# A fused attention and transformer kernel: where the softmax maximum is injected, how probabilities are stored, and leaner first-stage copies

## The chip, the cores and the metric

The kernel runs on one core of one Trainium2 chip. The metric is the time of one execution on the device in microseconds (us), the median of three runs. A profile is one further execution, recorded by the hardware profiler; its span runs from the first to the last instruction of the program.

The engines' names are as in the profile: PE is the matrix engine's matmuls and PEld its weight loads, DVE the vector engine, ACT the scalar engine (activations), POOL the GpSimd engine, SP the engine that issues the DMAs.

## The reference

The input x is 16 sequences of 256 tokens with 128 features. Two residual blocks follow each other. The first is one windowed attention (windows of 64 tokens, 16 heads of 8 features). The second is six layers, each of an attention (16 heads of 64 features, windows of 32 that look back at one window) and a feed-forward part with a gated gelu. Cut to what matters here:

```
x = x + first_attention(layernorm(x))          # _L0_attn_ref
    q, k = layernorm over the 8 features of a head;  softmax(q k^T) v;  W_proj, b_proj
x = x + six_layers(layernorm(x))               # _L0_ffn_ref
    for i in range(6):
        s = shift_tokens(x)                    # half of the features from the token before
        q, k, v = s @ Wqkv[i];  q, k = l2norm, scaled;  rotary tables
        p = softmax(8 * q k^T, masked to the window and the one before)
        x = (p v) @ Wo[i] + x
        s = layernorm(shift_tokens(x))
        x = (a * gelu(gate)) @ W2[i] + b2[i] + x      # a, gate = split(s @ W1[i] + b1[i])
```

## The kernel before

**Two stages.** `first_attention` computes the first block for all sequences and leaves the result, normalised and transposed, in `xg` in SBUF. Then the layers run, 6 x 32 tiles of 128 tokens, in one software pipeline.

**The pipeline of the layers.** Each tile passes through stages, and in turn t the kernel works on several tiles at once: `stage_p` (projections) on tile t, `stage_s` (scores) on t-1, `stage_e` (exponentials) on t-2, `stage_v` (probabilities times values) on t-3, `stage_w` (output projection) on t-5, and pieces of `stage_f` (feed-forward, one unit of two sequences in four turns) behind. Every stage is a generator that is cut into steps, and each step has a place in the turn between 0 and 1 (`AT_P`, `AT_E`, `AT_V`, `AT_W`, `AT_S`, `AT_F`, `AT_L`, lines 27 to 30). `merge_at` runs the steps sorted by place; equal places go in the order of the list of stages. `mul` (line 291) and `flip` (line 294) issue every matmul and transpose of the layers and pin each behind the one before, so that the order of the matrix engine is exactly this order. The other engines' orders are chosen when the program is built, by the priority of the program's order and by a model of when inputs are ready; they are in-order queues on the chip.

**The steps of a turn**, with the names used here:
- P0 to P5: the six projections (q, k in P0 to P3, k first; v in P4 and P5), each three matmuls, with four transposes among them that `turned` has queued: k and q of tile t-1 in P0 to P3, the probabilities p of tile t-2 in P4 and P5. Each projection takes a PSUM bank of the pool `p`, which has two; in P0 to P3 DVE multiplies it with the rotary tables (line 643), ACT squares it (line 652), then DVE reduces (653), and POOL adds and scales (654, 660, 664).
- S at .72: a mask matmul and 128 score matmuls into two banks of the pool `s` (two banks), then on DVE the negated row maxima `nm` (line 738).
- E at .2 and .21 of the next turn: a matmul per bank adds the maxima to the scores, and ACT writes the exponentials to `p` (one buffer, line 275 through `tab`).
- P4, P5 then transpose `p`, and ACT copies it to `pt` (line 621), one buffer of 8 x 128 columns, the half `mb` at a time.
- V1 at .1 and V2 at .45 of the turn after: 64 small matmuls each. V1 takes its two banks from the pool of four (`t`, `w`, `f`), V2 from the pool of the scores (`USE_V`). DVE takes reciprocals and multiplies (790, 791), ACT casts (795), POOL subtracts (796), and a DMA transposes the result.
- W at .47: 24 matmuls, added to `xg` by DVE (817).
- Feed-forward steps: Fc and Fo (centring and variance), six Fp (three gelus, three products), F2 (second matrix, added to `xg` by DVE, 895), and in the last layer `emit_out`: eight transposes of `xg` per unit into two banks of the pool `p`, each half added on DVE (834) to the residual. Before the gelus and after them ACT loads another table.

The order on the matrix engine around the change, in a turn without feed-forward steps, is S, P5, then P0, V1, P1, E, P2, V2, W, P3, P4.

**The first attention.** Eight units of 512 tokens pass `stage_load`, `stage_qkv`, `stage_heads`, `stage_soft`, `stage_out`, `stage_norm`, merged in a similar manner, but without pins. The lines that the change touches: `row_stats` sums rows by ACT (line 320, each with a read of the accumulator) for the units' first statistics (`a`) and the last ones (`b`); `rv` (370) is on DVE; `stage_heads` splits q and k into a high and a low half-precision part by ACT (414) and POOL (415) and doubles both by a DVE copy (417, 419) before a DMA transpose; `stage_out` fills one bank per half c of the rows (480), with a reciprocal (482) and two multiplications (485) each. Its five PSUM pools have 2, 2, 2, 1, 1 banks.

Of the kernel before, what the change touches and what calls it, by code (L numbers as in the profile page):

```python
# [10 lines left out]
F32 = mybir.dt.float32  # L11
# [3 lines left out]
AF = mybir.ActivationFunctionType  # L15
ALU = mybir.AluOpType
AX = mybir.AxisListType
# [7 lines left out]
KT = 2  # L25
LAG_S, LAG_P, LAG_V, LAG_W = 1, 2, 3, 5
AT_P = tuple(c / 6 for c in range(6))
AT_E, AT_V, AT_W, AT_S = (0.2, 0.21), (0.1, 0.45), (0.47,), (0.72,)
AT_F = ((0.86,), (0.06, 0.74, 0.88), (0.03, 0.27, 0.8), (0.1, 0.35, 0.6))
AT_L = 0.71  # L30
LOAD_AT = 6
LOAD_T = 10
SPLIT = (2, 4, 2)
SPLIT0 = (2, 2, 2, 1, 1)
USE = dict(p=0, t=1, w=1, f=1, s=2)
USE_V = (1, 2)
LQ0, LH0, LS0, LO0, LN0 = 2, 4, 6, 7, 9
# [11 lines left out]
VPRE = 16.0  # L49
# [6 lines left out]
def kernel(  # L56
# [233 lines left out]
    def mul(*args, **how):  # L290
        pin(T.matmul(*args, **how))  # L291
# [5 lines left out]
    def first_attention(p1, p2, p3, pqp, psp0, pop, pyp, ptp=None):  # L297
# [17 lines left out]
        def row_stats(xt, pre):  # L315
            mu = p3.tile([128, 4], F32, name=f"{pre}mu")
            rs = p3.tile([128, 4], F32, name=f"{pre}rs")
            sq = p3.tile([128, 128], F32, name="sq0")
            for t in range(4):
                S.activation(sq, xt[:, t], AF.Copy, scale=-1.0 / 128.0, accum_out=mu[:, t : t + 1])  # L320
            for t in range(4):
                S.activation(sq, xt[:, t], AF.Square, bias=mu[:, t : t + 1], accum_out=rs[:, t : t + 1])
            rsqrt(rs, rs, 1.0 / 128.0)
            return mu, rs
# [39 lines left out]
        def stage_load(u):  # L364
            if u:
                load_x(u)
            e = U[u]
            _, e.rs = row_stats(e.xt, "a")
            e.rv = p1.tile([128, 4], F32, name="rv")
            V.tensor_scalar(e.rv, e.rs, VPRE, None, ALU.mult)  # L370
            yield
            e.xnt = p1.tile([128, 2, 4, 128], FR, name="xnt")
            pt = ptp.tile([128, 4, 128], F32, name="pt" if ptp is not pyp else "py")
            for t in range(4):
                T.transpose(pt[:, t], e.xt[:, t], ident)
            S.copy(e.xnt[:, 0], pt)
            V.tensor_tensor(e.xnt[:, 1], pt, e.xnt[:, 0].bitcast(F32), ALU.subtract)
            G.tensor_tensor(e.xt, e.xt, bpt.unsqueeze(1).to_broadcast([128, 4, 128]), ALU.add)
            yield
# [26 lines left out]
        def stage_heads(u):  # L406
            e = U[u]
            e.hl = []
            for s in range(2):
                src = e.qk[:, :, s * 128 : s * 128 + 128].rearrange("p t (h d) -> p t h d", d=8)  # L410
                hl = p1.tile([128, 4, 16, 4, 8], HP, name=f"hl{s}")
                for t in range(4):
                    hi, lo = hl[:, t, :, 0], hl[:, t, :, 2 if s else 1]
                    S.copy(hi, src[:, t])
                    G.tensor_tensor(lo, src[:, t], hi, ALU.subtract)
                    if s:
                        V.tensor_copy(hl[:, t, :, 1:4:2], hl[:, t, :, 0:3:2])
                    else:
                        V.tensor_copy(hl[:, t, :, 2:4], hl[:, t, :, 0:2])
                tr = p2.tile([128, 4, 4, 128], HP, name=f"tr{s}")  # L420
                nc.sync.dma_start_transpose(
                    tr.rearrange("p t i q -> p (t i) q"), hl.rearrange("p t h a d -> p (t h a d)")
                )
                e.hl.append(tr)
                yield
# [41 lines left out]
        def stage_out(u, n2):  # L467
            e = U[u]
            for n in range(2):
                t = 2 * n2 + n  # L470
                pt0 = e.pt[n]
                v = v0[(4 * u + t) % NV0]
                o0 = p3.tile([128, 2, 8, 8], F32, name="o0")
                for c in range(2):
                    r = slice(64 * c, 64 * c + 64)
                    po = pop.tile([128, 8, 18], F32, name="po")
                    for gm in range(8):
                        p = gm % 4 * 2 + gm // 4
                        for q, (a, b) in enumerate(((0, 0), (0, 1), (1, 0))):
                            T.matmul(po[:, p], pt0[r, a * 8 + gm], v[r, b, p], start=(q == 0), stop=(q == 2))  # L480
                    rc = p3.tile([128, 8], F32, name="rc0")
                    V.reciprocal(rc, po[:, :, 16])
                    for hp in range(2):
                        h = slice(64 * hp, 64 * hp + 64)
                        V.tensor_tensor(
                            o0[h, c],
                            po[h, :, hp * 8 : hp * 8 + 8],
                            rc[h].unsqueeze(2).to_broadcast([64, 8, 8]),
                            ALU.mult,
                        )  # L490
                yield
                py = pyp.tile([128, 512], F32, name="py")
                T.transpose(py[:, 0:128], o0.rearrange("p c a b -> p (c a b)"), ident)
                ot0 = p3.tile([128, 128], F32, name="ot0")
                S.copy(ot0, py[:, 0:128])
                py = pyp.tile([128, 512], F32, name="py")
                for c in range(2):
                    r = slice(64 * c, 64 * c + 64)
                    for hp in range(2):
                        T.matmul(  # L500
                            py[r, 0:128],
                            ot0[r, hp * 64 : hp * 64 + 64],
                            wp[r, hp],
                            start=(hp == 0),
                            stop=(hp == 1),
                        )
                V.scalar_tensor_tensor(e.xt[:, t], py[:, 0:128], 1.0 / VPRE, e.xt[:, t], ALU.mult, ALU.add)
                yield
# [49 lines left out]
    def bank(kind):  # L558
        n = USE.get(kind, kind)
        return banks[n].tile([128, 512], F32, name=f"bank{n}")  # L560
# [47 lines left out]
    def turned(src, dst, mb):  # L608
        hold = []

        def one(m):
            if m == 0:
                hold.append(bank("t").rearrange("p (m q) -> p m q", q=128))
            flip(hold[0][:, m], src(m), ident)
            if m == 3:
                to = dst
                if isinstance(dst, Tl):
                    if mb == 0:
                        dst.pt = work.tile([128, 8, 128], F32, name="pt", bufs=1)
                    to = dst.pt  # L620
                S.copy(to[:, mb * 4 : mb * 4 + 4], hold[0])  # L621

        turns.extend((lambda m=m: one(m)) for m in range(4))

# [63 lines left out]
    def line_up(t):  # L688
        if 0 <= t - LAG_S < total:
            d = tiles[t - LAG_S]  # L690
            if d.j == 0:
                kts[0] = front.tile([128, 8, 256], F32, name="kt", bufs=KT)
            d.ktp = kts[0]
            d.kt = d.ktp[:, :, 128 - 128 * d.j : 256 - 128 * d.j]
            d.qt = front.tile([128, 8, 128], F32, name="qt", bufs=2)
            for s, dst in ((1, d.kt), (0, d.qt)):
                for hb in range(2):
                    nat = d.nat[s][hb].rearrange("p (m a) d -> p m (a d)", a=2)
                    turned(lambda m, nat=nat: nat[:, m], dst, hb)
        if 0 <= t - LAG_P < total:  # L700
            d = tiles[t - LAG_P]
            for mb in range(2):
                turned(lambda m, mb=mb: d.p[:, mb * 4 + m].rearrange("p a k -> p (a k)"), d, mb)

# [60 lines left out]
    def stage_v(t):  # L765
        d = tiles[t]
# [11 lines left out]
        for mb in range(2):  # L778
            po = [bank(USE_V[mb])[:, 0:260].rearrange("p (m d) -> p m d", d=65) for a in range(2)]
            for m in range(4):  # L780
                for s in range(4):
                    for a in range(2):
                        r = slice(64 * a, 64 * a + 64)
                        q = slice(32 * s, 32 * s + 32)
                        mm = mb * 4 + m
                        mul(po[a][q, m], d.pt[r, mm, q], vv[s, a][r, mm], start=True, stop=True)
            of = work.tile([128, 4, 2, 64], F32, name="of", bufs=2)
            for a in range(2):
                rc = work.tile([128, 4], F32, name="rc", bufs=4)
# [30 lines left out]
    def emit_out(b, nb):  # L820
        g, k = divmod(b, GB)
        n = 2 * nb
# [4 lines left out]
        yt = pool.tile([128, 12 if name == "gt" else 4, 128], F32, name=name, bufs=bufs)[:, 0:n]  # L827
        for a in range(2):
            r = slice(64 * a, 64 * a + 64)
            pm = bank("p")[:, 0:256].rearrange("p (t c) -> p t c", c=64)[:, 0:n]  # L830
            for t in range(n):
                c0 = t % 2 * 128 + a
                flip(pm[:, t], xg[g][r, k + t // 2, c0 : c0 + 128], ident[r, r])
            V.tensor_tensor(yt[:, :, r], pm, r1[:, :, r], ALU.add)  # L834
# [187 lines left out]
```

## Time and profile before

| What | us |
|---|---|
| median of three runs (3214.35 to 3215.15) | 3214.44 |
| the profiled execution, its own time | 3213.12 |
| its span, first to last instruction | 3211.3 |
| first attention: start to the first scores of the layers | about 287 |
| first to last exponential of the layers | 293.3 to 3168.7 |
| TensorE clock granted, mean over the span | 0.957 |

The page has a line for each engine (busy time, share of the span, instructions) and rows of digits in which the span is cut into 40 slices: a digit is the busy share in tenths, and in the row PEclk the share of the clock that was granted. A busy time of the matrix engine is modelled at its ends and can hide short waits; therefore starts are compared in what follows. In a list of instructions the last bracket gives the idle time of the engine before it and who ended it.

### The profile page before, as it was taken

To read this page: it belongs to the slowest core of one execution; us is meant where nothing else is said; L and a number is where in the kernel's file an instruction comes from. 1 tells how busy PE (TensorE), PEld (TensorE's weight loads), DVE (VectorE), ACT (ScalarE), POOL (GpSimd) and SP (SyncE) were. 2 spreads that over 40 slices of the span, in tenths; PEclk is the share of its full clock that TensorE was granted. 3 is DMA by queue.
4 is the path that set the end of the run, shared out by engine and by line. 5 is a ranking of instruction groups with operands and counts; after the bars stand their busy time and mean duration, and the time that the engine had idled before them with its cause. 6 is when DMAs were issued, how large, how long until landed. Compare 5 with 4: busy or idle time off the path is not lost. (4 is left out here: it accounts for less than half of the span.)

```text
span 3211.3 us, 153330 instructions
## 1 busy us (share of the span) xinstructions
PE 2994.2 (93%) x67106; PEld 2099.0 (65%) x67106; DVE 2583.3 (80%) x4850; ACT 2384.4 (74%) x5034; POOL 2510.2 (78%) x2578
## 2 busy tenths in 40 slices
PE   4887999999999999999999999999999999999997
PEld 3655766666666666666666666666666666666664
DVE  7987888887788887788887788887788887787774
ACT  6877777777777777777777777777777777776774
POOL 5656988888888788888788888788888788887772
PEclk6558999999999999999999999999999999999998
DMA  4763545444444434444444444444444444443433
GB/s 109 134 130 86 101 96 106 89 85 88 93 95 107 87 87 88 93 95 105 89 87 86 94 96 104 89 88 84 95 98 103 89 89 81 95 93 91 89 89 71
DMA packets 622945, 302.98 MB, mean 94 GB/s; under 512 B 533446, under 2 KB 545732, under 8 KB 622276
## 3 DMA queue, kind: packets, MB, share of 16 engines
q1 hardware_dynamic: 622276, 293.18, 43.5%
q8 instruction: 528, 8.65, 1.1%
q14 instruction: 141, 1.16, 0.1%
HBM read 22.45 MB, written 4.19 MB: 8 GB/s over the span
## 5 line engine op out<-in xcount | busy, mean ns | idle before, releaser
L291 PE MATMUL bank<-wqkv,xhl 128*128 128x512 f16 x3456 | 1234.4, 380 | 10.0 <-ACT sq L652 9.3
L654 POOL TENSOR_TENSOR sum<-mc 128x512 f32<-128x512 f32 x768 | 995.8, 1300 | 230.4 <-DVE mc L643 211.3
L643 DVE TENSOR_TENSOR mc<-bank,tq 128x1024 f32<-128x1024 f32 x768 | 928.2, 1218 | 148.3 <-PE bank L294 135.4
L664 POOL TENSOR_TENSOR sum<-sum,r 128x512 f32<-128x512 f32 x768 | 796.2, 1058 | 31.9
L653 DVE TENSOR_REDUCE r<-sq 128x8 f32<-128x512 f32 x768 | 520.4, 683 | 277.4 <-ACT sq L652 267.4
L294 PE MATMUL bank<-ident,sum 128*128 128x128 f32 x3072 | 710.5, 273 | 0.0
L796 POOL TENSOR_TENSOR ohl<-of,ohl 128x512 f16<-128x512 f32 x384 | 451.7, 1176 | 211.5 <-ACT ohl L795 210.8
L652 ACT ACTIVATE sq<-bank 128x512 f32<-128x512 f32 x768 | 459.6, 608 | 160.4 <-DVE mc L643 158.7
L294 PEld LDWEIGHTS bank<-ident,sum 128*128 128x128 f32 x3072 | 432.4, 141 | 131.8 <-issue 13.9
L291 PEld LDWEIGHTS <-xhl 128*128 128x128 f16 x3456 | 337.6, 98 | 191.0 <-issue 18.5
L795 ACT CAST ohl<-of 128x512 f16<-128x512 f32 x384 | 237.8, 619 | 269.5 <-DVE of L791 266.8
L291 PE MATMUL bank<-vb,pt 64*32 64x65 f32 x6144 | 376.0, 225 | 50.9 <-ACT p L275 26.4
L291 PEld LDWEIGHTS bank<-vb,pt 64*32 64x32 f32 x6144 | 257.0, 105 | 218.6 <-ACT p L275 75.1
L294 PE MATMUL bank<-ident,p 128*128 128x128 f32 x1536 | 355.0, 273 | 0.1
L291 PE MATMUL bank<-v,pt 64*32 64x65 f32 x6144 | 312.6, 224 | 39.4 <-ACT p L275 17.8
L291 PE MATMUL bank<-vw,pt 64*32 64x65 f32 x12288 | 331.8, 225 | 1.2 <-issue 1.0
L791 DVE TENSOR_TENSOR of<-bank,rc 128x256 f32<-128x256 f32 x768 | 295.4, 416 | 1.7
L291 PE MATMUL bank<-ot,wohl 128*128 128x128 f16 x4608 | 292.0, 220 | 2.0 <-issue 1.1
L291 PEld LDWEIGHTS bank<-kt,qt 64*32 64x32 f32 x24576 | 255.4, 105 | 44.4 <-issue 44.1
L291 PE MATMUL bank<-kt,qt 64*32 64x64 f32 (+1 forms) x24576 | 283.7, 223 | 0.3 <-issue 0.2
L291 PEld LDWEIGHTS bank<-v,pt 64*32 64x32 f32 x6144 | 235.2, 105 | 70.5 <-ACT p L275 33.2
L291 PEld LDWEIGHTS <-wohl 128*128 128x128 f16 x4608 | 259.1, 98 | 21.0 <-issue 3.1
(155 smaller groups left out, 5033.9 us busy)
## 6 DMA issues: line engine op xcount, KB each, us to landing
v<-vb SPq DMA_DIRECT2D x384, 130.0 KB
vw<-vb SPq DMA_DIRECT2D x384, 130.0 KB
vw<-vb SPq DMA_DIRECT2D x576, 65.0 KB
wraw<-in_L_ffn_Wqkv_dram SPq DMA_DIRECT2D x36, 256.0 KB
wraw<-in_L_ffn_Wo_dram SPq DMA_DIRECT2D x12, 256.0 KB
ot<-ohl SPq DMA_TRANSPOSE x192
xt<-in_L_attn_x_dram SPq DMA_DIRECT2D x8, 256.0 KB
r1d<-xt SPq DMA_DIRECT2D x8, 256.0 KB
```

The source lines that it names most:

```text
L291: pin(T.matmul(*args, **how))
L294: pin(T.transpose(*args))
L643: V.tensor_tensor(prod, p4.unsqueeze(3).to_broadcast([128, 8, 2, 2, 32]), tq[:, s, d.j].unsqueeze(1).to_broadcast([128, 8, 2, 2, 32]), ALU ...
L652: S.activation(sq, pp.rearrange("p (h d) -> p h d", d=64), AF.Square)
L653: V.tensor_reduce(r[:, hb * 8 : hb * 8 + 8], sq, AX.X, ALU.add)
L654: G.tensor_tensor(mc, m2[:, :, 0], m2[:, :, 1], ALU.add)
L664: G.tensor_tensor(mc, mc, rb.unsqueeze(2).to_broadcast([128, 8, 64]), ALU.mult)
L791: V.tensor_tensor(of[:, :, a], po[a][:, :, 0:64], rc.unsqueeze(2).to_broadcast([128, 4, 64]), ALU.mult)
L795: S.copy(ohl[:, 0, h], of)
L796: G.tensor_tensor(ohl[:, 1, h], of, ohl[:, 0, h], ALU.subtract)
```

## The change

Six edits:
- the places of `stage_e` go from .2 and .21 to .09 and .095, which is before V1 (.1) and behind the feed-forward steps at .03 and .06;
- `pt` becomes two tiles of four times 128 columns, `pt0` and `pt1`, one buffer each;
- `emit_out` takes its banks from the pool of four;
- `stage_heads` writes high and low parts at double width by ACT and POOL, and the DVE copies are gone;
- `stage_out` uses one tile of two banks for both halves c, with the matmuls of the two halves alternating, one reciprocal and two multiplications over both; the pool has one such tile, and the pools' counts are 2, 2, 1, 1, 1;
- the last statistics (`b`) take their sums by one DVE reduction and a small POOL multiplication, and `rv` moves from DVE to POOL.

```diff
-AT_E, AT_V, AT_W, AT_S = (0.2, 0.21), (0.1, 0.45), (0.47,), (0.72,)
+AT_E, AT_V, AT_W, AT_S = (0.09, 0.095), (0.1, 0.45), (0.47,), (0.72,)
...
-SPLIT0 = (2, 2, 2, 1, 1)
+SPLIT0 = (2, 2, 1, 1, 1)
...
-            for t in range(4):
-                S.activation(sq, xt[:, t], AF.Copy, scale=-1.0 / 128.0, accum_out=mu[:, t : t + 1])
+            if pre == "a":
+                for t in range(4):
+                    S.activation(sq, xt[:, t], AF.Copy, scale=-1.0 / 128.0, accum_out=mu[:, t : t + 1])
+            else:
+                V.tensor_reduce(mu, xt, AX.X, ALU.add)
+                G.tensor_scalar(mu, mu, -1.0 / 128.0, None, ALU.mult)
...
-            V.tensor_scalar(e.rv, e.rs, VPRE, None, ALU.mult)
+            G.tensor_scalar(e.rv, e.rs, VPRE, None, ALU.mult)
...
+                hi, lo = (slice(0, 2), slice(2, 4)) if s else (slice(0, 3, 2), slice(1, 4, 2))
                 for t in range(4):
-                    hi, lo = hl[:, t, :, 0], hl[:, t, :, 2 if s else 1]
-                    S.copy(hi, src[:, t])
-                    G.tensor_tensor(lo, src[:, t], hi, ALU.subtract)
-                    if s:
-                        V.tensor_copy(hl[:, t, :, 1:4:2], hl[:, t, :, 0:3:2])
-                    else:
-                        V.tensor_copy(hl[:, t, :, 2:4], hl[:, t, :, 0:2])
+                    two = src[:, t].unsqueeze(2).to_broadcast([128, 16, 2, 8])
+                    S.copy(hl[:, t, :, hi], two)
+                    G.tensor_tensor(hl[:, t, :, lo], two, hl[:, t, :, hi], ALU.subtract)
...
-                for c in range(2):
-                    r = slice(64 * c, 64 * c + 64)
-                    po = pop.tile([128, 8, 18], F32, name="po")
...
+                both = pop.tile([128, 2, 512], F32, name="po")
+                po = both[:, :, 0:144].rearrange("p c (m e) -> p c m e", e=18)
+                for gm in range(8):
+                    p = gm % 4 * 2 + gm // 4
+                    for q, (a, b) in enumerate(((0, 0), (0, 1), (1, 0))):
+                        for c in range(2):
+                            r = slice(64 * c, 64 * c + 64)
+                            T.matmul(po[:, c, p], pt0[r, a * 8 + gm], v[r, b, p], start=(q == 0), stop=(q == 2))
+                rc = p3.tile([128, 2, 8], F32, name="rc0")
+                V.reciprocal(rc, po[:, :, :, 16])
+                for hp in range(2):
+                    h = slice(64 * hp, 64 * hp + 64)
+                    V.tensor_tensor(
+                        o0[h],
+                        po[h, :, :, hp * 8 : hp * 8 + 8],
+                        rc[h].unsqueeze(3).to_broadcast([64, 2, 8, 8]),
+                        ALU.mult,
+                    )
...
-                    if mb == 0:
-                        dst.pt = work.tile([128, 8, 128], F32, name="pt", bufs=1)
-                    to = dst.pt
-                S.copy(to[:, mb * 4 : mb * 4 + 4], hold[0])
+                    dst.pt[mb] = work.tile([128, 4, 128], F32, name=f"pt{mb}", bufs=1)
+                    S.copy(dst.pt[mb], hold[0])
+                else:
+                    S.copy(dst[:, mb * 4 : mb * 4 + 4], hold[0])
...
-                        mul(po[a][q, m], d.pt[r, mm, q], vv[s, a][r, mm], start=True, stop=True)
+                        mul(po[a][q, m], d.pt[mb][r, m, q], vv[s, a][r, mm], start=True, stop=True)
...
-            pm = bank("p")[:, 0:256].rearrange("p (t c) -> p t c", c=64)[:, 0:n]
+            pm = bank("t")[:, 0:256].rearrange("p (t c) -> p t c", c=64)[:, 0:n]
```

More of the change, by code (lines that the diff above doesn't have):

```diff
@@ L473, in stage_out @@
                 o0 = p3.tile([128, 2, 8, 8], F32, name="o0")
-                for c in range(2):
-                    r = slice(64 * c, 64 * c + 64)
-                    po = pop.tile([128, 8, 18], F32, name="po")
[L477 to L490, printed above, removed]
+                both = pop.tile([128, 2, 512], F32, name="po")
[16 more added lines that the diff above has]
+                    )
                 yield
@@ L615, in one @@
             if m == 3:
-                to = dst
                 if isinstance(dst, Tl):
-                    if mb == 0:
-                        dst.pt = work.tile([128, 8, 128], F32, name="pt", bufs=1)
-                    to = dst.pt
-                S.copy(to[:, mb * 4 : mb * 4 + 4], hold[0])
+                    dst.pt[mb] = work.tile([128, 4, 128], F32, name=f"pt{mb}", bufs=1)
+                    S.copy(dst.pt[mb], hold[0])
+                else:
+                    S.copy(dst[:, mb * 4 : mb * 4 + 4], hold[0])
         turns.extend((lambda m=m: one(m)) for m in range(4))
@@ L701, in line_up @@
             d = tiles[t - LAG_P]
+            d.pt = [None, None]
             for mb in range(2):
```

## The prediction

> **What bounds the kernel now.** I read the page first, then stretches cut at turns, then the waits, then the engines' instructions in order of time.
>
> ```profile
> PE 2994.2 (93%) x67106; PEld 2099.0 (65%) x67106; DVE 2583.3 (80%) x4850; ACT 2384.4 (74%) x5034; POOL 2510.2 (78%) x2578
> PEclk6558999999999999999999999999999999999998
> ```
>
> TensorE is near full from slice 5 on, at the full granted clock; in the first three and a half slices (the first attention) it has about half the clock and is not full. So there are two stages with two limits. Here are four successive turns of the layers, cut where S (the scores) ends: a plain one, one with Fc/Fo, one with gelus, one with F2 (columns: stretch, length, busy us and count of PE, PEld, DVE, ACT, POOL, clock, DMA share, GB/s).
>
> ```profile
> 1567.57:1580.69 13.12, 12.96 (x342) 10.03 (x333) 12.01 (x23) 9.65 (x21) 11.07 (x13) 1.00 0.55 94
> 1580.69:1595.57 14.88, 14.21 (x336) 9.77 (x331) 12.30 (x23) 11.20 (x24) 11.15 (x12) 1.00 0.46 92
> 1595.57:1613.02 17.45, 16.08 (x351) 10.83 (x341) 11.92 (x22) 14.85 (x29) 14.33 (x16) 1.00 0.38 81
> 1613.02:1629.62 16.60, 16.60 (x350) 11.56 (x345) 15.55 (x28) 9.88 (x21) 12.97 (x13) 1.00 0.47 90
> ```
>
> DVE leaves 1.1 us free in the plain turn and in the F2 turn, 2.6 and 5.5 in the others. TensorE's order is written out, so a stall of it lengthens the turn at once. The waits between 300 and 3165 us say what it stalls on (in all, times, longest):
>
> ```profile
> PEld bank L291 <- ACT p L275: 104.5, 237, 0.7
> PEld bank L291 <- ACT pt L621: 45.4, 52, 1.0
> PE bank L294 <- DVE gt L834: 9.4, 6, 1.6
> ```
>
> The first is V2: its two banks come from the pool of the scores and are free only when both exponentials (p, L275) have read them. One such case, in the Fc turn, ScalarE then TensorE:
>
> ```profile
> 1587.14 0.59 ACT L621 COPY kt<-bank 128x512 f32<-128x512 f32 x1 [0.29 <-PE bank L294]
> 1587.83 0.62 ACT L865 CAST xnhl<-gt 128x512 f16<-128x512 f32 x1
> 1588.35 1.08 ACT L275 ACTIVATE p<-bank 128x512 f32<-128x512 f32 x2
> ```
> ```profile
> 1586.94 0.59 PE L291 MATMUL bank<-nm,identh 128*128 128x512 f16 x2
> 1587.37 0.38 PE L291 MATMUL bank<-wqkv,xhl 128*128 128x512 f16 x1
> ...
> 1588.99 0.30 PE L291 MATMUL bank<-vb,pt 64*32 64x65 f32 x2 [0.37 <-ACT p L275]
> ...
> 1590.26 1.51 PE L291 MATMUL bank<-ot,wohl 128*128 128x128 f16 x24
> ```
>
> E is issued at 1586.94, its exponentials end at 1589.43, and V2 starts only with the first (1588.99) and takes 1.27 us.
>
> To count the stalls I took, for each block of TensorE, the distance from its start to the next block's start, less the short distance that recurs for it: P 1.09, V 0.79, E 0.43, W 1.35, S 1.71, Fp 0.65 us. Over 188 turns the excess is 225 us. At V2: 1.02 us in each of 46 Fc turns, 0.80 in 46 gelu turns, 0.33 in 50 plain turns, none in 46 F2 turns (F2 covers it): 46.9 + 37 + 16.4 = 100 us. At V1: 85 us, of which 1.27 per gelu turn (the copy of pt and a gelu must empty its banks) and 0.37 per F2 turn. All else: 40 us.
>
> **E moves ahead of V1.** Nothing is added or removed: E (0.43) stands before V1 instead of after P1, 0.79 + 1.09 = 1.88 us earlier, so the exponentials may start that much earlier. E needs the two maxima (nm, L738). In the trace the second ends before the place where E will stand by a median of 1.08 us in plain, 2.6 in Fc, 3.4 in gelu and 0.94 in F2 turns; it would be late in 14% of F2 turns, 0.07 us on the mean. Behind E wait V1 and P1. By kind of turn:
> - Fc: E at 1585.06, exponentials after Fo's Ln, P0's square and Fo's Exp (until 1586.86), so over by 1588.0; V2 would come at 1585.06 + 0.43 + 0.79 + 2 x 1.09 = 1588.46. The 1.02 goes. But P4 then wants P2's bank at 1591.7, whose square ended at 1592.01: 0.3 back. 0.72 x 46 = 33.
> - gelu: P2 can't come before P0's square (1604.21), which follows the gelus and a table load, so E hiding in V1's wait brings nothing by itself. If the exponentials follow that square at once, W starts at 1606.13 instead of 1607.02 (0.89); if V1's cast (L795) stays ahead, 0.47. Mean 0.68 x 46 = 31.
> - plain: 0.33 to be had; ScalarE now idles 0.54 and 0.60 before and after P0's square, so there is room, but DVE is at 12.01 of 13.12. I take 0.2 x 50 = 10.
> - F2: E fills V1's 0.37; DVE at 15.55 of 16.60 lets me take half: 8.5.
>
> Sum 83; bounds: all of it, 46.9 + 0.89 x 46 + 16.4 + 17 = 121, and none. What is late next: P2 to P5, whose two banks wait for DVE's product (1.218) and the square behind it (0.608), 1.83 against two projections of 1.09. Other small stalls are 40 us over 188 turns, 0.2 each; I add half as much again: 0.1 x 188 = 19. **Net 64 us less.**
>
> **pt in two tiles**: nothing. In plain turns V1 starts while the second copy still runs (median start 3.97 after S began, copy over at 4.6), so there is no wait between halves to remove; the wait of 45.4 us above falls in gelu turns, where V1's bank is the one that this copy empties. Were it the tile, up to 0.61 x 46 = 28 us would be V1's, but P2's wait for P0's square would hold it.
>
> **emit_out in the pool of four.** Six turns have the 8 output transposes. They take 2.43 us there; 0.84 in the drain, where nothing is queued. The 9.4 us above is the second half waiting for one of the projections' two banks. 1.6 + 0.2 (neighbouring P) = 1.8 x 6 = 10. In the other pool the bank before is w's or F2's, whose readers must be done anyway. Bounds 0 and 11.
>
> **The drain.** E at .2 falls between two gelus there and costs two extra table loads of 1.28 us; at .09 it comes before them. 4 us, bounds 0 and 8.
>
> **The first attention.** In 60 to 240 us DVE is busy 161.0, ACT 136.4, POOL 112.4 of 180 us. DVE comes first. DVE's part:
>
> ```profile
> L417 DVE COPY hl<-hl 128x256 f16<-128x256 f16 x32 | 14.5, 468 | 0.2
> L419 DVE COPY hl<-hl 128x256 f16<-128x256 f16 x32 | 13.3, 449 | 5.3 <-POOL hl L415 5.2
> L485 DVE TENSOR_TENSOR o<-po,rc 64x64 f32<-64x64 f32 x128 | 28.0, 219 | 1.9
> L482 DVE RECIPROCAL rc<-po 128x8 f32<-128x8 f32 x64 | 12.6, 200 | 9.1 <-PE po L480 8.3
> L370 DVE TENSOR_SCALAR rv<-ars 128x4 f32<-128x4 f32 x8 | 4.1, 518 | 1.8 <-ACT ars L302 1.8
> ```
>
> Copies: -27.8. L482: half of 64: -6.3. L485: 64 at 0.286 (L507, 128 columns out of PSUM) instead of 128 at 0.219: -9.7. L370: -4.1. The new tensor_reduce over 512 columns: 8 x 0.683 (L653) = +5.5. DVE: 42 us less. ScalarE: 32 sums with their reads (0.304 + 0.191) go, -15.8; 64 copies double, at most to 0.467 (L388) and at least by the slope of 0.59 to 1.045 us for 512 more columns, 0.11 each: +7 to +11. POOL: 64 subtractions go from 0.431 to 0.657 (L595, same types, 256 columns) = +14.5, and 16 small ones at 0.25 (L660) = +4. The interleaved po matmuls (1536, 29 ns apart now) can only come closer; one po tile instead of two makes the next wait for three DVE operations (0.8), some 6 us after it was filled: covered. If DVE's 42 all counted, 42 less; but of that 161/235 or 29 falls in 60 to 240 us (DVE is busy 235 in the first 287), and ACT, some 6 lower, would then fill 130 of 151. I take **15 less**: a third, bounds 35 less and 5 more (POOL's added 18.5 in the chain to the head transposes, less what overlaps).
>
> One row speaks of a hidden cost: L419's copy at 163.06 took 1.68 us while POOL's L462 ran from 162.52 to 164.65; its shortest is 0.17. The Trainium skill, "SBUF — State Buffer", section "Who interferes with whom", says that DVE and GpSimd share a port pair which the first to issue holds for its whole instruction, and that a DVE operation with two SBUF inputs is blocked by a GpSimd one that reads SBUF. By it POOL's longer subtractions speak against the change: DVE's L310, L311, L313 and L401 (21.7 of 287 us) could meet 18.5 more us of POOL, an estimate of 1.4 us back, and the sum would be 14 instead of 15.
>
> **Sum.** 64 + 10 + 4 + 15 = 93 from the profiled execution's 3213.1 us (span 3211.3): 3120. The median of the runs is 1.3 above that execution: **3121 us**.
>
> **Rivals.**
> - A, ScalarE runs the exponentials ahead of P0's square. Then P0's bank is free 1.1 us later and P2 stalls in V2's place: 0.7 in a plain turn (slack 0.4), 0.1 in an Fc turn, 1.45 in a gelu turn; 2.25 x 47 = 106 of the 121 given back. 3213 - 15 - 29 + 1 = 3170. For it: ScalarE idles 0.54 before that square. Against: the square is older in the program.
> - B, slower: DVE runs P0's rotary product before the maxima. E then waits 1.22 + 0.68 = 1.9 us in plain and F2 turns (slack 1.08 and 0.94), V1 and P1 behind it: 96 x 1.9 = 182 lost against 74 kept elsewhere, 3322. It decides from about 40 of the 96 turns on. For it: the maxima are late already in some F2 turns. Against: they now directly follow a reduction and leave DVE idle after them.
> - C, the wait does not vanish but moves wholly to P2 to P5 (DVE 15.55 of 16.60), and only the other parts remain: 3213 - 29 + 1 = 3185.
>
> **How the numbers follow.** Forecast 0.58, with its own range of 3075 to 3160; A 0.21; C 0.10; B 0.11. The range runs from 3070 (143 us less: most of all the upper bounds) to 3190 (C held, B left out). This kernel can tell 0.2%, 6.4 us, from no change. Faster 0.86, same 0.03 (the worst of C with nothing from the first stage), slower 0.11.
>
> **What would show it.** V2's wait on p near 0; exponentials within 1 us of E's end; E without a wait on nm; the first exponential of the layers some 15 us earlier than 293 us; output transposes near 0.9 us; DVE's busy time in the first 287 us some 40 us lower. A wait of P2 on the square, or of E on nm, over 30 us would make the prediction wrong, as would a first stage that ends later than now.

## The result, and the profile after

The changed kernel takes 3256.84 us (median of four, 3254.82 to 3259.22) against 3214.8 for the kernel before: a ratio of 1.013, with a 95% interval of 1.0113 to 1.0148. It is 42 us slower, where 93 less was forecast. Its profiled span is 3257.4 us.

Cut at the starts of S, the time moved like this. The first scores of the layers come at 274.1 instead of 287.5 us, 13 earlier. From there to the last scores it takes 2929.6 instead of 2867.9 us, 62 more, although the output transposes save some 10 in it. From the last scores to the end it takes 53.7 instead of 56.0. So the loss is in the layers, and it is some 72 us large.

The page of the kernel after, engines and granted clock:

```profile
PE 2991.2 (92%) x67106; PEld 2067.5 (63%) x67106; DVE 2582.4 (79%) x4690; ACT 2380.6 (73%) x4968; POOL 2529.1 (78%) x2594
PEclk5558999999999999999999999999999999999998
```

Only POOL is busy for longer, by 19 us, and its new work is in the first attention; in the layers the clock is 1.00 in both. The 46 us of span are waiting. Four successive turns, cut as in the prediction (plain, Fc, gelu, F2):

```profile
1712.68:1724.70 12.02, 12.02 (x307) 8.90 (x301) 10.49 (x20) 8.67 (x20) 9.65 (x12) 1.00 0.53 104
1724.70:1740.19 15.49, 14.75 (x353) 9.91 (x343) 11.97 (x23) 12.01 (x26) 12.63 (x13) 1.00 0.41 88
1740.19:1757.66 17.47, 15.64 (x380) 10.77 (x364) 11.99 (x23) 14.72 (x28) 13.54 (x15) 1.00 0.32 71
1757.66:1773.66 16.00, 15.98 (x348) 10.63 (x339) 13.62 (x25) 9.55 (x20) 12.89 (x14) 1.00 0.39 86
```

On the mean over all turns of a kind, cut at the starts of S, plain turns went from 12.38 to 12.41 us, Fc turns from 14.82 to 15.70, gelu turns from 16.82 to 17.54, F2 turns from 16.50 to 16.18 (most of this in the six with output transposes; 16.23 to 16.11 without them). The loss is in the Fc and gelu turns. The waits between 300 and 3165 us of the kernel after say what is late (us in all, times, longest):

```profile
DVE r L654 <- ACT sq L653: 327.5, 365, 2.7
...
PEld L291 <- DVE of L793: 62.9, 128, 0.9
PE bank L291 <- ACT sq L653: 59.1, 63, 1.3
PEld bank L291 <- ACT gt L858: 46.4, 43, 1.9
...
PE bank L291 <- DVE nm L740: 0.2, 1, 0.2
```

and the same rows of the kernel before:

```profile
DVE r L653 <- ACT sq L652: 266.4, 336, 1.7
...
PEld bank L291 <- ACT gt L856: 15.1, 26, 1.5
...
PE bank L291 <- ACT sq L652: 2.1, 3, 0.8
...
PEld L291 <- DVE of L791: 1.1, 4, 0.3
```

V2's wait for the exponentials is gone from the list, as intended: by the distances between starts its excess fell from 100 to 16 us. E does not wait for the maxima (0.2). In their place TensorE waits for P0's square (before P2, in gelu turns), for the square of Fc's result (L858, before Fo), and for V2's multiplications, which hold the banks that S wants. Counted from start to start, P2 in gelu turns begins 1.33 us later behind the block before it (61 us in all), Fo 0.64 later behind P0 (29 us), and the S that ends an Fc turn 0.64 later behind P4 (29 us). Counted in one way for both kernels the total excess is 314 us instead of 239 (the prediction's own count was 225); the 75 more match the loss. And DVE stands 61 us longer in front of the square of a projection.

That last row is the one to look into. DVE in a plain turn, before (its reduction of P0's square is the fourth row):

```profile
1569.91 1.22 DVE L643 TENSOR_TENSOR mc<-bank,tq 128x1024 f32<-128x1024 f32 x1 [0.64 <-PE bank L294]
1571.17 0.25 DVE L790 RECIPROCAL rc<-bank 128x4 f32<-128x4 f32 x2
1571.39 0.42 DVE L791 TENSOR_TENSOR of<-bank,rc 128x256 f32<-128x256 f32 x1
1571.80 0.69 DVE L653 TENSOR_REDUCE r<-sq 128x8 f32<-128x512 f32 x1
1572.41 0.41 DVE L791 TENSOR_TENSOR of<-bank,rc 128x256 f32<-128x256 f32 x1
```

and after:

```profile
1776.00 1.23 DVE L644 TENSOR_TENSOR mc<-bank,tq 128x1024 f32<-128x1024 f32 x1 [0.49 <-PE bank L294]
1777.28 0.25 DVE L792 RECIPROCAL rc<-bank 128x4 f32<-128x4 f32 x2
1778.23 0.69 DVE L654 TENSOR_REDUCE r<-sq 128x8 f32<-128x512 f32 x1 [0.70 <-ACT sq L653]
1778.83 0.74 DVE L793 TENSOR_TENSOR of<-bank,rc 128x256 f32<-128x256 f32 x2
```

Before, the reciprocals and one multiplication of V1 fill the time in which ScalarE squares P0, and the reduction finds its input ready. After, both multiplications stand behind the reduction, and DVE waits 0.70 us. Two orders changed for this, both chosen when the program was built. On DVE the reduction moved ahead of the multiplication. On ScalarE both exponentials moved ahead of P0's square in plain, gelu and F2 turns, and the first of them in Fc turns, as here:

```profile
1729.79 0.69 ACT L275 ACTIVATE gt<-bank,epst 128x512 f32<-128x512 f32 x1 [0.53 <-PE bank L291]
1730.37 0.59 ACT L275 ACTIVATE p<-bank 128x512 f32<-128x512 f32 x1
1730.85 0.60 ACT L653 ACTIVATE sq<-bank 128x512 f32<-128x512 f32 x1
1731.32 0.61 ACT L275 ACTIVATE p<-bank 128x512 f32<-128x512 f32 x1
```

Counted over all turns, what stands on DVE ahead of P0's reduction in plain and F2 turns, and how long that reduction waits on the mean (us, plain / Fc / gelu / F2):

| Kernel | ahead of the reduction | wait |
|---|---|---|
| before | both reciprocals, one multiplication | 0.18 / 1.14 / 0.99 / 0.12 |
| after | both reciprocals | 0.91 / 2.10 / 0.58 / 0.59 |

Over the 50, 46, 46 and 46 turns the difference is 36.5 + 44 - 19 + 22 = 84 us of DVE. That this is what the layers lose is not shown by the count. How such a wait can travel is seen in one case, from a plain turn into the Fc turn behind it: V2's multiplications are late, ScalarE's cast waits for them, the square of a projection stands behind the cast, DVE's reduction waits for the square, ScalarE's root (`r`) for the reduction, and the square of Fc's result (L858), which Fo needs, comes last:

```profile
1722.39 0.74 DVE L793 TENSOR_TENSOR of<-bank,rc 128x256 f32<-128x256 f32 x2
1723.17 0.62 ACT L797 CAST ohl<-of 128x512 f16<-128x512 f32 x1 [0.86 <-DVE of L793]
1725.13 0.62 ACT L653 ACTIVATE sq<-bank 128x512 f32<-128x512 f32 x1
1725.78 0.69 DVE L654 TENSOR_REDUCE r<-sq 128x8 f32<-128x512 f32 x1 [0.89 <-ACT sq L653]
1726.56 0.31 ACT L275 ACTIVATE r<-r,tiny 128x16 f32<-128x16 f32 x1 [0.81 <-DVE r L654]
1727.96 0.61 ACT L858 ACTIVATE gt<-bank 128x512 f32<-128x512 f32 x1
```

### The profile page after: what moved, and what is told of

It is laid out like the page before. It is cut to its first block, busy times and chain, and to the rows that moved or that the text cites. A ratio compares the mean times of both kernels' runs of the same rounds, so it can differ in the third digit from the quotient of the medians.

```text
span 3257.4 us, 153052 instructions
## 1 busy us (share of the span) xinstructions
PE 2991.2 (92%) x67106; PEld 2067.5 (63%) x67106; DVE 2582.4 (79%) x4690; ACT 2380.6 (73%) x4968; POOL 2529.1 (78%) x2594
## 5 line engine op out<-in xcount | busy, mean ns | idle before, releaser
L291 PE MATMUL bank<-vb,pt 64*32 64x65 f32 x6144 | 336.6, 224 | 2.1 <-ACT pt L620 0.5
L793 DVE TENSOR_TENSOR of<-bank,rc 128x256 f32<-128x256 f32 x768 | 287.1, 415 | 1.6
L291 PE MATMUL bank<-xnhl,w1hl 128*128 128x512 f16 x864 | 237.3, 385 | 24.0 <-ACT gt L281 18.6
```

The costliest lines, as they stand in the source:

```text
L793: V.tensor_tensor(of[:, :, a], po[a][:, :, 0:64], rc.unsqueeze(2).to_broadcast([128, 4, 64]), ALU.mult)
```

## The experiments

**Which part.** Five kernels split the change. In the first, the changed kernel gets its old places of E back (the reverse edit of the first line of the change):

```diff
-AT_E, ... = (0.09, 0.095), ...
+AT_E, ... = (0.2, 0.21), ...
```

> The changed kernel with E back at .2 and .21, all else as changed. Theory: the place of E costs some 72 us (the 61.7 us that the layers lost between the first and the last scores, plus the 10 us that the output transposes won inside that stretch), and the other edits are worth what was forecast (13 us in the first attention, 10 us at the outputs, 2 to 4 in the drain). Then this run is at 3256.8 - 72 = 3185 us, within 10. Rival: the probabilities in two tiles, or the new order of the first attention's leftovers, cost part of the loss; then this run stays above 3215.

Measured 3190.48 us, ratio 0.9919 (0.9904 to 0.9933). The second is the kernel before with E's places at .09 and .095 alone.

> The kernel before with E at .09 and .095 and nothing else. Theory: it loses the same 72 us by itself, 3214.8 + 72 = 3287 us, and the scalar engine runs the exponentials ahead of P0's square, so that P2 waits for it in gelu turns (1.3 us each). Rival: E at .09 harms only together with two pt tiles; then this run is between 3200 and 3220.

Measured 3285.11, ratio 1.0218 (1.0203 to 1.0234). So E's place costs 70 us on the kernel before and 66 on the other parts, and the other parts bring 24. Of these parts each was then made alone on the kernel before: `emit_out`'s bank, `pt` in two tiles, and the edits of the first attention.

> The kernel before with the output transposes in the pool of four and nothing else. Theory: the turns with output transposes lose 1.6 to 1.8 us each, six of them: 3214.8 - 10 = 3205 us. Rival: the four banks are then short for the probabilities' transposes and the gain is returned there: 3213 to 3217 us.

> The kernel before with the probabilities in two tiles and nothing else. Forecast: nothing, 3214.8 within 4 us. Rival: V1 no longer waits for the second half's copy and 10 to 28 us go.

> The kernel before with the edits of the first attention alone. Forecast: the layers are as before and the first scores come 13 us earlier, 3201 us, within 4. Rival: the layers' order changes with it and takes part of that back, 3208 us or more.

Measured: `emit_out` 3202.59, ratio 0.9961 (0.9946 to 0.9976); `pt` 3217.14, 1.0002 (0.9993 to 1.0011); first attention 3204.5, 0.9967 (0.9954 to 0.998). That is 12, 0 and 11 us less.

**Is it ScalarE's order?** The changed kernel, with both exponentials pinned behind P0's square of the same turn:

```diff
+            made = tab(d.p[:, :, a], pss[a], AF.Exp, scale=SDIV)
+            if t + LAG_P < total:
+                behind(made, tiles[t + LAG_P].squares[0])
```

> The changed kernel with one ordering edge more: on the scalar engine the exponentials come behind P0's square. Theory: the order square after exponentials is what costs; P2's wait in gelu turns (1.33 us x 46 = 61 us) goes, and the 2.4 us for which the vector engine waits for the square in Fc turns shrinks; the run is between 3160 and 3195 us. Rival: what costs is E ahead of V1 on the matrix engine or the vector engine's load, whatever the scalar engine's order; then the run is above 3240 us.

Measured 3242.99, ratio 1.0087 (1.007 to 1.0104): 14 us back of 66, the rival. DVE's waits did not fall, because the order that was built for it changed again: now the reciprocals too stand behind the reduction, which waits 0.66 us in plain and F2 turns. A second try put only E's matmuls at .09 and .095, and its exponentials at .2 and .21 behind the square, the cast of V1 and a transposed copy:

```diff
+            yield
+        for a in range(2):
+            behind(tab(d.p[:, :, a], pss[a], AF.Exp, scale=SDIV), *ahead.values())
```

> The changed kernel with E's two matmuls still at .09 and .095, but the exponentials issued at .2 and .21 and held behind the last square of P0, the last cast of V1's values and the last copy of transposed keys: on the scalar engine the old order, on the matrix engine the new one. Theory now: the matrix engine's order costs nothing, what costs is the exponentials in front of other work of the scalar engine (the square 14 us by the run before, the cast and the copy the remaining 50 or so); then this run is at 3185 to 3200 us, as with E at .2. Rival: E ahead of V1 on the matrix engine delays V1 and what hangs on it; then 3230 us or more.

Measured 3314.34, ratio 1.0306 (1.0289 to 1.0323). The exponentials were too late now: TensorE's waits for them, 104.5 and 41.1 us in the kernel before, are 222.4 and 151.7. In plain and F2 turns DVE again had P0's reduction ahead of V1's reciprocals. So this run decides nothing about E's place.

**Is it E ahead of V1?** The changed kernel with E between V1 and P1, at .15 and .155:

> The changed kernel with E at .15, between V1 and P1. On the scalar engine the order is then the one of the run with the square first (square, exponentials, cast, copy), on the matrix engine V1 comes before E. If the scalar engine's order is the whole cause, this run is like that one, 3235 to 3250 us; if E ahead of V1 is, it is like E at .2, 3180 to 3200 us.

Measured 3176.44, ratio 0.9878 (0.9863 to 0.9892), faster than both kernels. ScalarE's order in its plain turns is that of the run of 3243 us, so it looked as though E ahead of V1 were the cause. But the built order of DVE differs too: reciprocals and one multiplication stand ahead of the reduction, as in the kernel before. The next five runs separate place and order. Each pins DVE's instructions of a turn by a list, with `mc` for the rotary products, `r` for the reductions, `rc` and `of` for V's reciprocals and multiplications, `fx` and `fl` for the feed-forward multiplication and subtraction. The rest is still placed when the program is built, and a little of it moves along: in F2 turns ScalarE's cast of V1's values and its copy of transposed keys change places. The edit:

```diff
+    def keep_order(t):
+        chain = [seen[n] for n in ORDER[kind].split() if n in seen]
+        for a, b in zip(chain, chain[1:]):
+            behind(b, a.ins)
```

First the version with E at .15, given the order of the run of 3243 us (in plain turns `mc0 r0 rc00 rc01 of00 of01 mc1 ...`; the order in F2 and Fc turns changes too):

> The kernel with E at .15 (3176 us), and on the vector engine the order that the run with E at .09 and the square first has. Theory A (the vector engine's order is the cause): 3225 to 3260 us. Theory B (V1's lateness is): 3170 to 3195 us.

Measured 3246.58, ratio 1.0094 (1.0078 to 1.0111): DVE's order alone loses the 70 us, with V1 in time. Then the reverse, the run of 3243 us given the order of the version with E at .15 (`mc0 rc00 rc01 of00 r0 of01 mc1 ...`):

> The changed kernel with the square first (3243 us), and on the vector engine the order of the products, reductions, reciprocals and V's multiplications that the run with E at .15 has: in plain and F2 turns V1's reciprocals and first multiplication before P0's reduction, in Fc turns the old place of the feed-forward multiplications. Theory A: with E ahead of V1 the builder puts P0's reduction before V1's work, and the vector engine then stands still for the square (334 us in all instead of 249); with the order put back the run is at 3170 to 3195 us. Theory B: V1 itself comes 0.5 us too late, and the vector engine would then wait for it instead; the run stays at 3225 us or more.

Measured 3227.07, ratio 1.0036 (1.0023 to 1.0049): only 16 us back, which is in theory B's range. But the list for the Fc turn had made a wait of its own: it put the feed-forward multiplication ahead of V1's, while ScalarE made that multiplication's input behind the exponentials, and the Fc turns took 16.31 us. Without that, the feed-forward multiplication staying behind V1's:

```diff
-        fc="mc0 r0 rc00 rc01 fx of00 of01 mc1 fl mc2 ...",
+        fc="mc0 r0 rc00 rc01 of00 of01 fx mc1 fl mc2 ...",
```

> This is the changed kernel with P0's square ahead of the exponentials and the vector engine's order of the version with E at .15 in the plain, gelu and F2 turns (V1's reciprocals ahead of P0's reduction); in the Fc turns the feed-forward multiplication stays behind V1's multiplications, so that the wait seen with the whole order put back (3227, Fc turns of 16.31 us) can't arise. Theory A, the vector engine's order in these three kinds of turn and that one wait are the whole loss: Fc turns near 14.3 to 14.8, DVE waiting for the square near 250 us, time 3175 to 3195. Theory B, V1's results coming 0.5 us later cost by themselves, since the vector engine then waits for V1 where it waited for the square: time 3215 to 3235, with the vector engine's wait for P's square below 270 us and its waits for V1's banks longer than in the version with E at .15.

Measured 3183.53, ratio 0.9904 (0.9888 to 0.9921): theory A in the time and in DVE's wait for the square (247.9 us), though the Fc turns took 15.0 us, above its 14.3 to 14.8. The list still changed two things, the place of V1's reciprocals in plain and F2 turns and the order of the Fc turn, so each was put back alone.

> The changed kernel with P0's square ahead of the exponentials and its own order on the vector engine (3243), but in the plain and F2 turns V1's reciprocals stand ahead of P0's reduction, as in the version of 3183.5 us; the Fc turns keep their own order, in which two rotary products stand ahead of the feed-forward subtraction. Theory R, the reciprocals behind the square are the loss: 3185 to 3200, with the vector engine's wait for the square near 250 us. Theory F, the Fc turn's order is the loss: 3230 to 3245. If both carry it: about 3215, and the two runs' gains add up to some 60.

> The reverse: plain and F2 turns keep the order of the version of 3243 us (P0's reduction ahead of V1's reciprocals), and in the Fc turns the feed-forward subtraction stands ahead of the second rotary product and the reduction of P1 ahead of V2's reciprocals, as in the version of 3183.5 us. Theory R: 3230 to 3245, the wait for the square staying near 300 us or more. Theory F: 3185 to 3200. Both: about 3215.

Measured 3182.13, ratio 0.9892 (0.9877 to 0.9907) for the reciprocals, and 3245.48, ratio 1.0088 (1.0071 to 1.0105) for the Fc turn. Theory R: the Fc turn's order is worth nothing. In the first of the two the order within the Fc turns is untouched, and yet they are where more than half of the gain lies: they take 14.38 us on the mean instead of 15.14 in the run of 3243 us, F2 turns 16.72 instead of 17.32. So the wait in a plain turn is paid for in the turn behind it. In the waits of the run with the reciprocals put ahead, DVE's wait is below that of the kernel before:

```profile
DVE r L672 <- ACT sq L670: 249.3, 265, 1.9
```

Two places of E by two orders of DVE, medians in us, show it best. In all four kernels P0's square stands ahead of both exponentials on ScalarE, in every turn of their traces:

| | V1's reciprocals and one multiplication ahead of P0's reduction | behind it |
|---|---|---|
| E at .15, behind V1 | 3176.4 | 3246.6 |
| E at .09, ahead of V1 | 3182.1 | 3243.0 |

The order is worth 61 us with E at .09, where it differs in plain and F2 turns alone, and 70 with E at .15, where the list changes Fc turns too. The place is worth 4 to 6 in either direction, and there the intervals of the ratios overlap.

**Can the turns' best lengths be had together?** F2 turns took 16.2 us with E at .2 and 17.0 with E at .15, so the version with E at .15 got .2 and .21 in these:

```diff
+            (LAG_P, (0.2, 0.21) if (t - LAG_W - 3) % 4 == 3 else AT_E, stage_e),
```

> E at .2 and .21 in the turns with F2 and at .15 in the others. With E at .15 the F2 turns take 16.9 us, with E at .2 16.2, and the other turns are shorter by 0.1 to 0.5 at .15. If the turns' lengths can be had one by one, 46 x 0.7 = 32 us go: 3145 us. If the F2 turn only takes up what the turns before it left waiting (the vector engine's load), 3170 to 3185 us.

Measured 3173.75, ratio 0.9869 (0.9854 to 0.9884), the best of all, but 3 us better and not 30. E does stand behind P1 in these turns now, and yet they take 16.96 us on the mean, where it was 16.97: E's place in them is not what makes them long. An Fc, a gelu and an F2 turn together take 47.9 us with E at .2 everywhere (3190.5), 47.8 at .15 and 47.8 here, which fits the second reading: the F2 turn takes up what the two before it have left waiting.

## Why the prediction was wrong

- **The step that failed is "E moves ahead of V1", net 64 us less.** In place of -64 the runs show +66 to +70. Its gain at V2 came true: V2's excess fell by 83 us, and "Sum 83" had been forecast (8.5 of it at V1). What failed is the term for what is late next, 19 us for "other small stalls". In the changed kernel some 150 came up: 61 at P2 in gelu turns, 29 at Fo, 29 in front of S, the rest in smaller pieces. The step began with "Nothing is added or removed" and then moved only what stands on the matrix engine and the exponentials, with DVE's order taken as it stood in the trace. The same document says that the orders of the other engines are chosen when the program is built, from the program's order and a model of readiness; moving E changes that model's input, and both came out differently.
- **What it missed on DVE.** It saw that "DVE is at 12.01 of 13.12" in a plain turn and took this for a reason to gain less (0.2 of 0.33). It did not ask what DVE does while ScalarE squares P0: it does V1's reciprocals and a multiplication. With the multiplication behind the reduction, and the exponentials ahead of the square, DVE stands still for 0.91 us in plain and 0.59 in F2 turns of the changed kernel; with the reciprocals behind it too, and the square first, for 0.66 in both. The delay goes on into the next turn, to the square of Fc's result and Fo.
- **ScalarE's order was rival A's mechanism**, judged unlikely because "the square is older in the program". It came true in plain, gelu and F2 turns, and the prediction's own sign of being wrong with it: TensorE's wait for the square is 59.1 us, where over 30 was named. A's price for P2 was near in gelu turns (1.33 us measured, 1.45 forecast) and too high in plain ones (0.18, 0.7). Pinning the square back gave only 14 us. That run changed DVE's order along with it, so the price of ScalarE's order at a fixed order of DVE was not measured.
- **The gain does not stay even with the orders put back.** That kernel (3182.1) is 8 us better than E at .2 with the same other parts (3190.5), where 64 was forecast; in the profiled executions 2 of them lie between the first and the last scores (2855.6 against 2857.8 us) and 5.5 behind the last (51.6 against 57.1). V2's excess is some 80 us lower there too, but 57 came up between the start of S and the first Fp of the feed-forward turns, 17 in front of S and 16 at P2 in gelu turns. 44 of the 57 are in S itself, at the start of gelu turns: its first two matmuls start 0.96 us apart there (0.00 in the run of 3190.5 us), since the second bank waits for V2's multiplications on DVE in the Fc turn before.
- **Rival B did not occur**: E's wait for the maxima is 0.2 us in all. **Rival C** has the right shape, a wait that moves on, and with the orders put back its time comes out (3182 us, 3185 forecast), but its place was wrong: P2 to P5 are only one of three places.
- **The other terms held.** Outputs: forecast -10, measured -12; the transposes go from 2.43 to 0.40 us per turn. `pt`: forecast nothing, measured 1.0002. Drain: forecast -4, -2 between the last scores and the end. First attention: forecast -15, -13 by the first scores, -11 alone, though not by the working that was given, as follows.

The groups of the first attention after the change answer to those shown of before:

```profile
L420 POOL TENSOR_TENSOR hl<-qk,hl 128x256 f16<-128x256 f32 x64 | 41.9, 692 | 0.6 <-ACT hl L419 0.5
L419 ACT CAST hl<-qk 128x256 f16<-128x256 f32 x64 | 20.5, 407 | 1.3 <-POOL qk L407 1.3
L487 DVE TENSOR_TENSOR o<-po,rc 64x128 f32<-64x128 f32 x64 | 18.3, 286 | 1.2
L484 DVE RECIPROCAL rc<-po 128x16 f32<-128x16 f32 x32 | 8.1, 252 | 11.1 <-PE po L482 10.9
```

The copies are gone (-27.8), the multiplications went from 28.0 to 18.3 (forecast -9.7), the reciprocals from 12.6 to 8.1 (forecast -6.3). POOL's subtraction takes 692 ns, where 657 was taken, and ScalarE's cast 407 instead of 294, which is the lower of the two bounds (0.11 us more each). But DVE's busy time up to the first scores went from 235.4 to 210.4 us, 25 less and not 42. That a third of 42 reaches the end was a guess; half of 25 did, and that the sum came out near is luck.

Part of what DVE did not save stands in the four lines to which the prediction applied the Trainium skill's "SBUF — State Buffer", section "Who interferes with whom". Their instructions are the same in both kernels. Before and after:

```profile
L401 DVE TENSOR_TENSOR qk<-qk,sm 128x1024 f32<-128x1024 f32 x8 | 10.7, 1335 | 0.1
L311 DVE TENSOR_TENSOR rqb<-rqb,rqa 128x128 f32<-128x128 f32 x8 | 4.1, 511 | 0.1
L313 DVE TENSOR_TENSOR sm<-rqb,rqa 128x128 f32<-128x128 f32 x8 | 3.6, 451 | 0.1
L310 DVE TENSOR_TENSOR rqb<-rqb,rqa 128x128 f32<-128x128 f32 x8 | 3.3, 416 | 0.7 <-ACT rqa L309 0.6
```
```profile
L405 DVE TENSOR_TENSOR qk<-qk,sm 128x1024 f32<-128x1024 f32 x8 | 12.0, 1496 | 0.1
L313 DVE TENSOR_TENSOR sm<-rqb,rqa 128x128 f32<-128x128 f32 x8 | 5.6, 701 | 0.1
L310 DVE TENSOR_TENSOR rqb<-rqb,rqa 128x128 f32<-128x128 f32 x8 | 4.9, 617 | 0.7 <-ACT rqa L309 0.7
L311 DVE TENSOR_TENSOR rqb<-rqb,rqa 128x128 f32<-128x128 f32 x8 | 4.0, 504 | 0.1
```

That is 21.7 us before and 26.5 after, 4.8 more where the estimate by that rule was 1.4; the run with the edits of the first attention alone has the same 26.5. Of the 16 instructions of L310 and L311, those that no POOL instruction overlaps take 0.28 us in both kernels (14 before, 6 after), the others 1.74 and 0.73 on the mean. So these traces agree with the rule, and the estimate was too low.

**What stays open.** Why the place of E by itself is worth so little once the orders are right was followed only to where the waits reappear. The list of the run of 3183.5 us shortens the wait between S and Fp in gelu turns (excess 0.95 to 0.32 us, against the run of 3182.1) and lengthens those from P3 to S in Fc turns (0.40 to 1.05) by as much, which fits a DVE that is behind in both, but no run made DVE's work less to test it. Nor was the loss of the changed kernel itself divided between ScalarE's order and DVE's: putting both back takes all of it away, and ScalarE's alone takes 14 us.

## What to carry to other kernels

When one engine's order is written out by hand and the others' are chosen at build time, a move on the first is also a change of the others: before pricing it, list for each of the other engines what it does in front of each instruction that waits, and ask what remains if that filler comes later. Here an engine that is 79% busy, with its waits spread over each turn, could set the pace, and one instruction on the wrong side of its fillers cost 61 us of 3243. After such a move, compare the order of every engine with the old one, and pin the few that matter.

## What was not expected of the hardware

The clock that was granted in the first stage did not matter to its time. In the profiled execution of the run of 3173.75 us it was 1.00 between 60 and 240 us, in that of the run of 3176.44 us 0.50, with the same edits in this stage:

```profile
60.00:240.00 180.00, 137.37 (x2664) 100.05 (x2658) 151.62 (x313) 140.99 (x344) 128.65 (x104) 1.00 0.75 137
60.00:240.00 180.00, 137.74 (x2662) 99.98 (x2656) 151.50 (x311) 140.53 (x344) 128.49 (x104) 0.50 0.75 137
```

The first scores come at 274.3 and 274.5 us, and matmuls of 128x384 columns (L391) follow each other after 0.32 us in both. Whether these matmuls do not depend on that clock or the row does not show what they got, no run tells.

Doubling the width of a cast on ScalarE (128 to 256 columns) cost 38% (294 to 407 ns), on POOL's subtraction 61% (431 to 692 ns), so here one wide instruction is cheaper than two on either.
